# Four graph layers on one core: zero matmuls, the place of one group of transposes, and the loading of weights

## The chip, the cores and the metric

The kernel runs on one core of a Trainium2 chip. The metric is the device time of one execution in microseconds (us). One execution handles sixteen graphs.

## The reference

Sixteen graphs of 1024 nodes with 128 features pass through four layers. Each layer first normalizes its input over the features and applies relu, and adds its output to its input. The adjacency matrix is sparse (about 1.6% of the entries and the diagonal are above zero) and comes as a dense matrix of floats.

```python
# layer 0: neighbour sums over the adjacency, divided by its row sums, then one linear map of [h, sums]
h = jnp.maximum(_layernorm(x), 0.0); x = x + relu(concat(h, (adj.T @ h) / degree) @ W0.T + b0)
# layer 1: the same sum with adj / row sums, one linear map, leaky relu
h = jnp.maximum(_layernorm(x), 0.0); x = x + leaky(((adj / degree) @ h) @ W1.T + b1)
# layer 2: two rounds of message passing, with a score for every pair of nodes
h = jnp.maximum(_layernorm(x), 0.0)
for l in range(2):
    a, b = h @ We1[l, :D], h @ We1[l, D:]
    hid = relu(a[:, None, :] + b[None, :, :] + be1[l])
    scores = sigmoid(hid @ We2[l] + be2[l])
    messages = (adj * scores) @ h
    y = h + relu(concat(h, messages) @ Wu1[l] + bu1[l]) @ Wu2[l] + bu2[l]
    h = layernorm(y) * gamma[l] + beta[l]
x = x + h
# layer 3: attention over the neighbours, softmax((Wh1 + Wh2.T) * (adj + I)), elu
```

## The kernel before

**Lanes.** The work of one graph is cut into three Python generators. `first` (lane a) does layers 0 and 1, the norm ahead of layer 2, and the lists of neighbours (`build`). `main` (lane m) does the two rounds of layer 2. `last` (lane c) does the second update of layer 2 and layer 3. While graph b is in `main`, graph b-1 is in `last` and graph b+1 in `first`. `weave` takes the next piece from the generator whose share of its expected time is smallest: each yields an estimate in us, divided by MAIN_US, FIRST_US or LAST_US. That gives the order in which instructions are written down. A scheduler then orders them on each engine by priority and its own estimate of readiness, and allots tiles from pools; each engine runs its own queue in order.

**Layer 2.** A pair of node blocks that share edges is gathered (`gather`, L1015) by matmuls of a one-hot matrix (`on`, `om`) with the two linear parts (`part`) into the PSUM tile `pre`, which has two buffers. ACT takes its relu (L1031), and DVE the rest that half precision loses (L1032); both are in the tile `hid`. `dots` (L1048) multiplies `hid` by the score weights into `sc`; `scores` transposes it (`pt`) and spreads it on the edges (`val`); `scatter` (L1131) turns this into the matrix `p`, DVE multiplies it by the adjacency (`upd`), and `message` (L1148) adds products of it to one of two message sums in PSUM (`msg`, 512 columns, tags acc0 and acc1). `between` updates a half of the nodes between the two rounds (`update`: h2, xn, tx, then a norm with the power on POOL at L242 and the scaling at L365).

**Zero matmuls.** A message sum is made of many products of different widths, in an order that the lanes decide. So the sum is first set to zero by a matmul of zeros (`zero`, L563), and every product adds to it. Layer 3 does the same with its three sums per graph (`hp`, L507; tiles of 387, 387 and 258 columns).

**Norms.** `pre_ln` computes mean and variance on DVE, the power on POOL (L242), then writes the relu of the scaled rows on ACT, eight instructions (L251), and `transposed` turns them on PE (L259) through PSUM back to SBUF on ACT (L260). The last norm in `first` writes the tile `xf`; its transpose goes to a DRAM copy, which `main` reads back later.

**The start.** All weights are loaded on ACT's DMA queue ahead of everything else. Then `run` lets `first` of graph 0 go up to layer 0's own products (`bb`), calls `scaled` (which folds the signs and sizes of We2 into We1 and finds a power of two that keeps the scores in range: `bound`, `bound_t`, `unit`, `be`, `w3T`, `v`), and goes on with `first`: for each of eight row tiles of the adjacency a load of rows (`at`) and of columns (`ct`), the transposes `tn`, the neighbour products `nb`, and a write of the transposed rows to DRAM (`adjT`). Rows and columns share five buffers here.

## Time and profile before

| | value |
|---|---|
| median of three runs | 5316.95 us (5308.2 to 5318.65) |
| span of the profiled execution | 5323.4 us |
| PE busy (matmuls) | 4977.0 us, 93% |
| DVE, ACT, POOL busy | 79%, 57%, 4% |
| first 133 us: PE busy, DMA busy | 81.2 us, 64% |
| zero matmuls (L563) | 112 |

A busy time is the time in which an instruction of the engine was under way; matmuls overlap, so their busy times are longer than their share of the queue. In a timeline a row holds the start, the length, the engine and line, the tiles written and read, and in brackets the idle time of that engine before the row and what ended it. Rows with "q" behind an engine's name are DMA issues. The clock row holds the share of its full clock that TensorE was granted.

### The profile page before, as it was taken

The numbers are of one execution on the slowest core, as the hardware profiler recorded it, in microseconds if no ns is written. First come the engines' busy times: TensorE is split into PE (matmuls) and PEld (weight loads), VectorE is DVE, ScalarE is ACT, GpSimd is POOL, SyncE is SP. The second block draws the span as 40 slices with busy tenths as digits, with TensorE's granted clock in tenths as the row PEclk, the third lists the DMA queues.
The fourth block names the chain that finished last, engine by engine and source line by source line (L and its number), as shares of the span: only waits on it lengthen the run. The fifth ranks groups of instructions, "written<-read, shape, count | busy, mean of one in ns | idle before, by whom it ended". The sixth has DMA issues, their size and how long they took to land.

```text
span 5323.4 us, 112270 instructions
## 1 busy us (share of the span) xinstructions
PE 4977.0 (93%) x45109; PEld 3739.4 (70%) x45109; DVE 4216.4 (79%) x9543; ACT 3044.9 (57%) x6790; POOL 189.3 (4%) x137
## 2 busy tenths in 40 slices
PE   6999999999999999999999999999999999999986
PEld 5766777777777777777777777777767777777664
DVE  4776787877879778797887978878797887978876
ACT  5556564655646556475564756656465564755543
POOL 0000000000000000000000000000000000000000
PEclk8999999999999999999999999999999999999998
DMA  6242425243252433424334242432524334243121
GB/s 185 64 143 88 123 62 150 83 127 108 75 147 74 134 94 89 141 73 125 96 107 130 62 138 88 121 115 72 154 71 136 97 89 142 74 126 93 57 63 48
DMA packets 740130, 554.47 MB, mean 104 GB/s; under 512 B 32273, under 2 KB 686353, under 8 KB 739601
## 3 DMA queue, kind: packets, MB, share of 16 engines
q1 hardware_dynamic: 734496, 545.58, 34.4%
q8 instruction: 356, 5.83, 0.5%
q10 hardware_dynamic: 5104, 1.65, 0.1%
q14 instruction: 174, 1.42, 0.1%
HBM read 446.44 MB, written 100.66 MB: 103 GB/s over the span
## 4 chain that ended last, share of the span: by engine, by line
PE 55%; DVE 22%; ACT 12%; DMA 5%; issue 3%; POOL 2%; SPq 0%; ACTq 0%; POOLq 0%; DVEq 0%
PE pre L1015 14%; PE p L1131 7%; DVE val L1106 7%; PE nb L289 6%; PE msg L1148 5%; PE bb L297 3%; PE sc L1048 3%; DVE hid L1032 3%; DMA at<-in_adj_dram 3%; PE h L343 3%; PE hp L507 3%; ACT hid L1031 2%; PE pq L873 2%; PE pn L829 2%; DMA a<-adjT 2%
## 5 line engine op out<-in xcount | busy, mean ns | idle before, releaser
L1031 ACT ACTIVATE hid<-pre 128x320 f16<-128x320 f32 (+1 forms) x2048 | 915.6, 455 | 666.8 <-PE pre L1015 603.0
L1032 DVE SCALAR_TENSOR_TENSOR hid<-pre,hid 128x320 f16<-128x320 f32 (+1 forms) x2048 | 1006.8, 505 | 240.6 <-ACT hid L1031 227.0
L1015 PEld LDWEIGHTS <-part 128*128 128x128 f16 x8192 | 746.0, 98 | 404.8 <-issue 196.6
L1015 PE MATMUL pre<-on,part 128*128 128x320 fp8e4 (+1 forms) x4096 | 985.2, 310 | 42.7 <-DVE hid L1032 32.5
L1015 PE MATMUL pre<-om,part 128*128 128x320 fp8e4 (+1 forms) x4096 | 962.9, 309 | 0.0
L1148 PE MATMUL msg<-upd,xf 128*128 128x128 f32 (+3 forms) x3008 | 595.3, 320 | 0.3 <-DVE upd L1139 0.3
L1106 DVE TENSOR_TENSOR val<-onT,u 128x768 f32<-128x768 fp8e4 (+1 forms) x576 | 561.1, 1010 | 3.1
L1131 PE MATMUL p<-val,omT 128*128 128x128 f16 x6528 | 507.3, 219 | 23.4 <-DVE val L1106 13.4
L1131 PEld LDWEIGHTS <-omT 128*128 128x128 fp8e4 x6528 | 423.0, 96 | 89.6 <-issue 62.3
L884 ACT ACTIVATE om<-pm 128x320 fp8e4<-128x320 f32 (+1 forms) x576 | 269.8, 468 | 292.0 <-PE pm L829 289.3
L1148 PEld LDWEIGHTS msg<-upd,xf 128*128 128x128 f32 x3008 | 410.3, 192 | 15.7 <-DVE upd L1139 1.6
L1106 DVE TENSOR_TENSOR val<-omT,u 128x768 f32<-128x768 fp8e4 x448 | 410.7, 950 | 0.0
L1139 DVE SCALAR_TENSOR_TENSOR upd<-p,adj 128x512 f32<-128x512 f32 x512 | 348.9, 681 | 74.9 <-PE p L1131 69.8
L1131 PE MATMUL p<-val,onT 128*128 128x128 f16 x4480 | 375.2, 219 | 2.4 <-DVE upd L1139 2.4
L869 ACT ACTIVATE onT<-pn 128x384 fp8e4<-128x384 f32 (+1 forms) x576 | 297.9, 517 | 120.9 <-PE pn L829 97.3
L507 PE MATMUL hp<-wh,e 128*128 128x129 f32 x2048 | 330.0, 283 | 14.3 <-DVE e L503 14.0
L1069 ACT ACTIVATE srow<-sc,be_s,down 128x128 f32<-128x128 f32 (+2 forms) x512 | 256.2, 541 | 142.6 <-PE sc L1048 140.2
L1131 PEld LDWEIGHTS <-onT 128*128 128x128 fp8e4 x4480 | 304.9, 97 | 46.7 <-issue 14.5
L507 PEld LDWEIGHTS hp<-wh,e 128*128 128x128 f32 x2048 | 282.5, 193 | 48.3 <-issue 19.7
L820 DVE TENSOR_SCALAR on<-far,wid 128x384 fp8e4<-128x384 f16 (+1 forms) x576 | 242.3, 427 | 67.2 <-PE pre L1015 59.5
L1048 PE MATMUL sc<-hid,slide 128*32 128x320 f16 (+1 forms) x4096 | 281.0, 317 | 14.6 <-DVE hid L1032 10.7
L816 ACT ACTIVATE far<-iota_off,mid 128x384 f16<-128x384 f16 x448 | 273.6, 629 | 7.8 <-DVE on L820 4.8
(217 smaller groups left out, 8118.5 us busy)
## 6 DMA issues: line engine op xcount, KB each, us to landing
at<-in_adj_dram SPq DMA_DIRECT2D x128, 512.0 KB, 3.9
ct<-in_adj_dram SPq DMA_DIRECT2D x128, 512.0 KB, 4.4
adjT<-tn SPq DMA_DIRECT2D x128, 512.0 KB, 5.2
l<-adjT SPq DMA_DIRECT2D x128, 512.0 KB, 4.3
adj<-adjT SPq DMA_DIRECT2D x256, 256.0 KB, 3.6
a<-adjT SPq DMA_DIRECT2D x128, 384.0 KB, 3.3
adj<-adjT SPq DMA_DIRECT2D x448, 64.0 KB, 2.3
adj<-adjT SPq DMA_DIRECT2D x192, 128.0 KB, 2.7
```

The source lines that it names most:

```text
L289: nc.tensor.matmul(ps, mat[:, k], z[:, k], start=(k == 0), stop=(k == T - 1))
L507: nc.tensor.matmul(sums[:, t], e[:, i, t * P : (t + 1) * P], wh[:, k + i, : D + 1], start=False, stop=True, skip_group_check=True,)
L816: nc.scalar.activation(far[:, : ck * P], self.iota[t == u][:, : ck * P], AF.Abs, bias=s.mid[:, i : i + 1])
L869: nc.scalar.activation(onT, pn[:, : ck * P], AF.Copy, saturate=False)
L1015: nc.tensor.matmul(pre[:, :c], path.parts[node // Q][:, k, node % Q, v], hot[:, :c], start=(hot is on and k == 0), stop=(hot is om and k = ...
L1031: nc.scalar.activation(hid[:, 0, :c], pre[:, :c], AF.Relu)
L1032: nc.vector.scalar_tensor_tensor(hid[:, 1, :c], pre[:, :c], 0.0, hid[:, 0, :c], op0=OP.max, op1=OP.subtract)
L1048: ins = nc.tensor.matmul(self.sc[g * G : (g + 1) * G, : self.c], self.path.slide[:, self.l, G - 1 - r : 2 * G - 1 - r], self.hid[self.done ...
L1106: nc.vector.tensor_tensor(pair[:, :, :ck], right, v.rearrange("p k i o -> p i k o").to_broadcast([P, 2, ck, P]), op=OP.mult,)
L1131: nc.tensor.matmul(self.ps[d][:, i], left[:, k], halves[:, k, :, h], start=(k, h) == terms[0], stop=(k, h) == terms[-1],)
L1139: nc.vector.scalar_tensor_tensor(upd, self.ps[d], S_SCALE, self.adj[:, d * Q : (d + 1) * Q], op0=OP.add, op1=OP.mult,)
L1148: nc.tensor.matmul(self.msg[h][:, (lo - h * Q) * P : (hi - h * Q) * P], self.xf[mb // Q][:, mb % Q], up, start=False, stop=True, skip_grou ...
```

## The change

Three things are changed.

1. The zero matmuls go. The first product into a message sum or a layer-3 sum carries the start flag, and later products are ordered behind it on PE (`add_to`, with `issue_after`). The tile of zeros goes too.
2. In `first`, the last norm and its transposes are taken apart: after the norm the generator yields 5 instead of 2, and the transposes are ordered behind the gather that was written down last at that point, except for graph 0. FIRST_US goes from 115 to 118.
3. Fifteen of the weight loads move into `load_rest`, called after layer 0's own products are written down, and `scaled` is called at the ninth piece of `first` that follows, not ahead of it.

```diff
-FIRST_US = 115.0
+FIRST_US = 118.0
...
+    def load_rest():
+
+        nc.scalar.dma_start(be2_bc, be2.rearrange("l o -> o l").broadcast_to([P, L]))
+        nc.scalar.dma_start(w3_sb, w3)
...
+    def add_to(opened, dst, left, right):
+
+
+        with ExitStack() as behind:
+            if opened is not None:
+                behind.enter_context(tc.issue_after(opened))
+            ins = nc.tensor.matmul(
+                dst, left, right, start=opened is None, stop=True, skip_group_check=True
+            )
+        return ins.ins if opened is None else opened
...
-                zero(sums)
                 sums = sums.rearrange("p (t d) -> p t d", d=D + 1)
+                opened = None
...
-                            nc.tensor.matmul(
-                                sums[:, t], e[:, i, t * P : (t + 1) * P], wh[:, k + i, : D + 1],
-                                start=False, stop=True, skip_group_check=True,
+                            opened = add_to(
+                                opened, sums[:, t], e[:, i, t * P : (t + 1) * P], wh[:, k + i, : D + 1]
                             )
...
-            ps = self.psum.tile([P, HALF], F32, tag=f"acc{h}", name=name)
-            self.zero(ps)
-            return ps
-
-        def zero(self, ps):
-            nc.tensor.matmul(ps, self.zero16, self.iota2[:, : ps.shape[1]], start=True, stop=True)
+            self.opened[h] = None
+            return self.psum.tile([P, HALF], F32, tag=f"acc{h}", name=name)
...
-            yield from lane.pre_ln(xt, f"2_{name}", dst=s.xf)
-            s.xT = self.kept(lane.hT, "xT", f"xT0_{b}")
+            lane.normal(xt, s.xf, AF.Relu, f"2_{name}")
+            yield 5
+
+            with ExitStack() as behind:
+                if b:
+                    behind.enter_context(tc.issue_after(self.gathered))
+                turned = lane.transposed(s.xf, f"2_{name}")
+            yield 2
+            s.xT = self.kept(turned, "xT", f"xT0_{b}")
...
+                    path.gathered = ins.ins
...
-                    nc.tensor.matmul(
-                        self.msg[h][:, (lo - h * Q) * P : (hi - h * Q) * P],
+                    self.path.opened[h] = add_to(
+                        self.path.opened[h], self.msg[h][:, (lo - h * Q) * P : (hi - h * Q) * P],
                         self.xf[mb // Q][:, mb % Q], up,
-                        start=False, stop=True, skip_group_check=True,
                     )
...
             first = self.first(0)
             next(first)
-            self.scaled()
-            for us in first:
+            load_rest()
+            for n, us in enumerate(first):
                 if us is None:
                     break
+                if n == 8:
+                    self.scaled()
```

## The prediction

> **What bounds the kernel now.** I read the page first: engine shares, then the clock row.

> ```profile
> PE 4977.0 (93%) x45109; PEld 3739.4 (70%) x45109; DVE 4216.4 (79%) x9543; ACT 3044.9 (57%) x6790; POOL 189.3 (4%) x137
> ...
> PE   6999999999999999999999999999999999999986
> ...
> PEclk8999999999999999999999999999999999999998
> ```

> PE is busy in 4977.0 of 5323.4 us, and below nine tenths only in the first slice and the last two. In between the kernel is bound by PE's queue, which runs in order. So time can be won in three ways: fewer matmuls, fewer waits in that queue, or a shorter first slice. The change tries all three.

> Next, the groups of instructions by form, for the matmuls that only write zeros:

> ```profile
> L563 PE MATMUL msg<-iota,zero 128*128 128x512 f16 x64 | 24.5, 386 | 6.4 <-DVE w_sb L155 6.4
> L563 PE MATMUL hp<-iota,zero 128*128 128x387 f16 x32 | 10.5, 327 | 0.4 <-ACT whr L283 0.4
> L563 PE MATMUL hp<-iota,zero 128*128 128x258 f16 x16 | 4.4, 273 | 0.0
> ```

> There are 112, with 39.4 us of busy time; but busy times of pipelined matmuls overlap, so their price is from start to start, in PE's timeline. The same timeline of graph 4 shows the wait that the moved transposes cause; ACT's and POOL's timelines show its origin:

> ```profile
> 1913.28 0.38 PE L563 MATMUL msg<-iota,zero 128*128 128x512 f16 x1
> 1913.50 0.57 PE L1015 MATMUL pre<-on,part 128*128 128x480 fp8e4 x2
> ...
> 1929.72 0.43 PE L1015 MATMUL pre<-on,part 128*128 128x320 fp8e4 x2 [0.74 <-DVE hid L1032]
> 1929.99 0.43 PE L1015 MATMUL pre<-om,part 128*128 128x320 fp8e4 x2
> 1932.82 0.33 PE L259 MATMUL tp<-ident,xf 128*128 128x128 f32 x1 [2.40 <-ACT xf L251]
> ...
> 1940.92 0.33 PE L563 MATMUL hp<-iota,zero 128*128 128x387 f16 x1
> 1941.08 0.30 PE L1015 MATMUL pre<-om,part 128*128 128x320 fp8e4 x1
> ```

> ```profile
> 1932.27 3.18 ACT L251 ACTIVATE xf<-x,st 128x128 f32<-128x128 f32 x8 [1.38 <-DVE st L249]
> ```

> ```profile
> 1930.40 1.64 POOL L242 TENSOR_TENSOR st<-st,half_neg 128x8 f32<-128x8 f32 x1 [31.77 <-DVE st L239]
> ```

> A zero matmul takes 0.22 us of the queue (1913.28 to 1913.50), the 387-wide one 0.16 us. At 1932.8 PE has nothing left ahead of a transpose whose operand is not there. The granted clock then falls, as a table of stretches shows:

> ```profile
> 1929.00:1934.80 5.80, 2.68 (x18) 1.26 (x18) 3.88 (x22) 2.96 (x8) 2.60 (x2) 1.00 0.00 0
> 1934.80:1938.30 3.50, 3.50 (x18) 2.75 (x16) 3.07 (x9) 2.70 (x6) 0.36 (x1) 0.51 0.39 116
> ```

> (The columns after the length are busy PE, PEld, DVE, ACT, POOL, then clock.) Last, the DMA issues of SP at the start, and a stretch of the first layer:

> ```profile
> 17.52 0.38 SPq L732 DMA_DIRECT2D x<-in_x_dram  x1
> 38.85 0.38 SPq L691 DMA_DIRECT2D ct<-in_adj_dram  x1
> ```

> ```profile
> 40.00:75.00 35.00, 26.27 (x200) 24.88 (x199) 8.81 (x25) 12.87 (x24) 0.00 (x0) 0.80 0.98 285
> ```

> From 17.5 to 38.9 us no load is issued, since the five row buffers are full until adjacency tile 0 is transposed; after that the DMA engines are 98% busy to 75 us. What starts these loads earlier ends them earlier.

> [...]

> **The change part by part.**

> *Zero matmuls.* All 112 go, with their weight loads and one memset. 64 x 0.22 + 32 x 0.16 + 16 x 0.11 (258 of 512 columns of 0.22) = 14.1 + 5.1 + 1.8 = 21.0 us. Two lie in the wait at the start and are free. In the orders of the two built programs the counts on each engine otherwise agree. Opening products add no work: they carry a start flag. The new order edges hold later products behind the opener on PE's own queue, where they stood anyway. The opener inherits the zero matmul's wait for its bank's reader, but later. I take 20, with 15 to 39 as ends: a third absorbed by waits, or the full busy time.

> *Weights and their folding.* Counting ACT's order, the scheduler still puts 19 of the 22 first issues ahead of the first norm; three go behind the transposed copies. ACT's last three issues end at 18.57; without three (0.33 to 0.49 us each, and gaps) the norm starts about 2 us sooner. It cannot start before about 12.4, when its statistics are done. The larger gain is on PE: before, the folding chain (bound at 30.2, unit at 33.8, be at 35.6) stands ahead of tile 0's transposes at 36.5. After, they stand among the bb products, which ran from 23.6 to 29.2. So their row is free near 29 instead of 38.85: 10 us less in front of a stretch that DMA bounds. The folding moves behind the third tile's neighbour products; its chain of about 5 us (30.2 to 35.6) makes PE wait there, but five rows of 0.5 MB at 285 GB/s are 9 us of loads in flight and hide it. ACT gets three issues among its copies, 1.3 us, and SP's order changes only between transposed writes and loads. Taken: 9; ends 2 (ACT's head start alone) and 12.

> *The transposes.* Where do they stand? Before, between last layer-1 product and first transpose, PE has 5.7 us of work (xn 1.72, pre 12 x 0.2 or 0.135, tx 0.48, hp 1.34); the wait is what is missing to the operand's chain. That chain, measured: product end 1923.63, transpose 1932.82, so 9.2 us: three additions on DVE (0.35, 1.23, 1.22), statistics 1.64, small ones 0.6, the power on POOL 1.64, ACT 0.5, and other DVE work between them. After, the yield of 5 puts the whole lane one product earlier against the main lane: ACT's eight xf stand ahead of the last diagonal hid, and 7.7 us of PE work precede the transpose (one h group of 1.72 and other places). The DVE work within the chain is alike (on, hid, on: 1.45, against on, bn pieces, hid: 1.65). So the first wait shrinks to 9.2 - 7.7 = 1.5 us, where before has 0.17 + 0.91 + 2.4 = 3.5.

> But ACT now issues the diagonal hid behind eight xf (3.18 us), and DVE handles its second half behind xf of the update (L365), which waits for POOL's power of st_y (1.0 to 1.3 us). The score products sc, queued on PE right behind the seventh transpose, start with that very hid. Walked with these durations: transposes from 14.3 (counted from the first gather of the round), seventh at 16.7, DVE's hid done at 19.2: a new wait of about 2.5 us. Behind it stand the last transpose and the next gathers. Together 4.0 to 4.5 us per graph against about 4.4 before (3.5, and 0.9 between the transposes). I take 0.

> Ends: all of it gone. The fourteen windows of 20 us around these waits have a clock of 0.91 (ten) or 0.83 (four): 10 x 1.8 + 4 x 3.4 = 32 us of lost clock, plus 14 x 3.5 = 49: minus 80. Worse by 1 us and another half-clock window (1.7) each: plus 38. FIRST_US 115 to 118 only compensates the longer yields; other small shifts of the lanes: plus or minus 10, since a graph has 15 us of PE waits in all.

> Sum: 20 + 9 + 0 = 29 us. On this execution's span, 5323.4 - 29 = 5294. The three timed runs are 5308.2 to 5318.65, median 5316.95, so the forecast is 5317 - 29 = 5288.

> **Rivals.**

> *The wait mostly goes (0.25).* If DVE reaches the hid early, the sc wait vanishes, and a 1.5 us wait alone may not cost the clock: 14 x (2 + 1.1 to 2.2) = 43 to 59 more, 5229 to 5245; all gone would be 5208. For it: that is where the new edge aims. Against: the order on ACT and DVE.

> *Less than forecast (0.17).* The gain at the start is hidden by the folding chain, or the wait grows by about 1 us: 5300 to 5317.

> *Slower (0.09).* One mechanism: sc waits behind L365, and so behind POOL. The 29 us are used up from 2.1 us more per graph; with 2.5 us more of this wait, and a half-clock window each: 14 x (2.5 + 1.7) = 59, less 29: 5347.

> *The change does not do what it says:* in part it does not (19 of 22 issues stay ahead); counted above.

> **Numbers.** The likeliest case has 0.49, 5274 to 5303 on its own. The range 5235 to 5313 leaves out most of the slower case and the far end of the first rival. A measurement can tell about 0.2%, 10.6 us. Below 5306: the likeliest, the first rival and a third of the second: 0.80; within 0.2%: 0.11; slower: 0.09.

> **What would show it.** No zero matmuls; the load of 38.85 issued near 29; PE's wait before the first xf transpose near 1.5 us, and one of about 2.5 us before sc. If the second is missing and the half-clock windows are fewer than fourteen, the first rival holds; if 9 us do not appear by 130 us, the start failed.

## The result and the profile after

The changed kernel takes 5272.67 us (median of 4 runs, 5270.28 to 5277.52) against 5317.11 us (5308.2 to 5318.65) for the kernel before: ratio 0.9921 with a 95% interval of 0.9904 to 0.9938, about 44 us less by the medians and 42 by the ratio. The forecast was 29 us less. The profiled execution spans 5272.1 us, the one of the kernel before 5323.4, which is 8 us above the median of that kernel.

The page of the changed kernel, in the rows that were shown of before:

```profile
PE 4924.4 (93%) x44997; PEld 3714.9 (70%) x44997; DVE 4225.4 (80%) x9542; ACT 3069.1 (58%) x6790; POOL 199.2 (4%) x137
...
PE   6999999999999999999999999999999999999986
...
PEclk8999999999999999999999999999999999999998
```

PE has exactly 112 matmuls fewer (45109 to 44997) (PEld likewise) and DVE one memset fewer; the other counts are the same. The bound is still PE's queue, with the first slice at 6. The clock row shows nothing at this grain, though the clock turns out to matter.

The sums in PSUM now have only products among their groups (line, operation, tiles, count, then busy time, mean, and idle time in front):

```profile
L195 PE MATMUL hp<-wh,e 128*128 128x129 f32 x2048 | 334.9, 285 | 14.5 <-DVE e L515 14.3
...
L195 PE MATMUL msg<-upd,xf 128*128 128x512 f32 x256 | 135.0, 609 | 0.0
```

Opening products have taken the place of the zero matmuls: 2048 products go into `hp` and 3008 into `msg`, as many as in before, and no row of zeros is left. Why one opening product is enough for a whole sum is not shown by these traces.

SP's DMA issues at the start:

```profile
14.53 0.38 SPq L738 DMA_DIRECT2D x<-in_x_dram  x1
26.38 0.38 SPq L697 DMA_DIRECT2D ct<-in_adj_dram  x1
```

The load that before issued at 38.85 goes out at 26.38, 12.5 us earlier (foretold: near 29). The folding chain now stands behind it on PE:

```profile
24.40 0.60 PE L760 MATMUL tn<-ident,at 128*128 128x128 f32 x4
...
34.71 1.05 PE L653 MATMUL bound<-lim_x,mag 128*128 128x1 f32 x8 [1.20 <-ACT mag L649]
36.28 0.27 PE L664 MATMUL bound_t<-ident,bnd 128*2 128x128 f32 x1 [0.52 <-DVE bnd L662]
38.20 0.58 PE L681 MATMUL unit<-sel,ones 2*128 2x4 f32 x2 [1.65 <-DVE sel L675]
```

The first relu of a gathered block on ACT comes at 125.9 us, in before at 136.4: 10.5 us earlier, where the forecast had 9. Over all fourteen traces of this document it comes at 136.4 to 138.8 us with the old start and at 125.1 to 127.0 with the new one.

Last, the moved transposes, in PE's and ACT's timelines of the graph that was shown of before:

```profile
1900.93 0.57 PE L1028 MATMUL pre<-om,part 128*128 128x480 fp8e4 x2
1902.60 0.33 PE L271 MATMUL tp<-ident,xf 128*128 128x128 f32 x1 [1.10 <-ACT xf L263]
...
1904.14 0.43 PE L1028 MATMUL pre<-om,part 128*128 128x320 fp8e4 x2
1906.23 0.55 PE L271 MATMUL tp<-ident,xf 128*128 128x128 f32 x3 [1.65 <-ACT hT L272]
1907.34 0.82 PE L1062 MATMUL sc<-hid,slide 128*32 128x480 f16 x8 [0.56 <-DVE hid L1046]
```

```profile
1902.06 3.19 ACT L263 ACTIVATE xf<-x,st 128x128 f32<-128x128 f32 x8 [1.55 <-DVE st L261]
1905.15 0.55 ACT L1045 ACTIVATE hid<-pre 128x480 f16<-128x480 f32 x1
1905.60 0.58 ACT L272 ACTIVATE hT<-tp 128x512 f32<-128x512 f32 x1
```

The wait in front of the first transpose is 1.10 us (forecast 1.5). A second one is there, but not where the forecast put it: not 2.5 us before `sc`, but 1.65 us before the fifth transpose, which waits until ACT has copied the first four out of PSUM (L272, 1905.60 to 1906.18), and ACT does that behind eight `xf` and a `hid`. Before `sc` 0.56 us are left. Together 3.31 us; before had 0.74 + 2.40 = 3.14 in the rows shown, and all fourteen graphs from the third on repeat these sums within 0.03 us. The wait was split, not removed. In the graph shown half clock still follows (a granted clock of 0.55 from 1907.8 to 1911.3 us); in ten of the fourteen graphs it does not.

What the split does to the clock is worked out from the clock records of each trace, over the stretch from graph 0's first relu of a gathered block to graph 15's. "Half-clock loss" is half the length of all stretches granted less than 0.9 (the records of before and after hold 1.0 and 0.5 alone); "PE idle" is the time in which no matmul was under way, and PE's own work is what is left of the stretch without these two. Before has 39.3 and 227.9 us there, after 22.2 and 235.0. The stretch is 44.5 us shorter (4848.3 to 4803.8): 17 from the clock, minus 7 more idle, and 34.5 in PE's own work, of which the zero matmuls by their start-to-start price are 21. That leaves some 13 us of faster interleaving. With 10.5 at the start and 3.8 lost in the last graph and behind it, this is the whole difference of the two executions, 51.3 us. Between the medians it is 44 us, so some 7 us of this sum belong to the one execution of before. The clock's 17 are in part such an item: over all recorded executions the granted clock is 0.984 in before and 0.986 in the changed kernel, some 10 us of the span. The forecast lacks both the clock and the interleaving.

### The profile page after: what moved, and what is told of

Read it like the earlier page. It is cut to its first block, busy times and chain, and to the rows that moved or that the text cites. A ratio compares the mean times of both kernels' runs of the same rounds, so it can differ in the third digit from the quotient of the medians.

```text
span 5272.1 us, 112168 instructions
## 1 busy us (share of the span) xinstructions
PE 4924.4 (93%) x44997; PEld 3714.9 (70%) x44997; DVE 4225.4 (80%) x9542; ACT 3069.1 (58%) x6790; POOL 199.2 (4%) x137
## 2 busy tenths in 40 slices
PE   6999999999999999999999999999999999999986
## 3 DMA queue, kind: packets, MB, share of 16 engines
q10 hardware_dynamic: 5104, 1.65, 0.1%
## 4 chain that ended last, share of the span: by engine, by line
PE 52%; DVE 23%; ACT 13%; DMA 7%; POOL 2%; issue 2%; SPq 0%; ACTq 0%; POOLq 0%; DVEq 0%
PE pre L1028 13%; DVE val L1120 6%; PE p L1145 6%; PE nb L301 6%; PE msg L195 4%; DMA at<-in_adj_dram 4%; PE sc L1062 3%; PE h L355 3%; DVE hid L1046 3%; PE bb L309 3%; PE hp L195 3%; DMA a<-adjT 2%; PE pq L886 2%; ACT hid L1045 2%; PE pn L842 2%
## 5 line engine op out<-in xcount | busy, mean ns | idle before, releaser
L1028 PE MATMUL pre<-on,part 128*128 128x320 fp8e4 (+1 forms) x4096 | 976.2, 308 | 22.2 <-DVE hid L1046 18.2
L195 PE MATMUL hp<-wh,e 128*128 128x129 f32 x2048 | 334.9, 285 | 14.5 <-DVE e L515 14.3
L301 PE MATMUL nb<-z,l 128*128 128x128 f32 x2048 | 270.8, 282 | 26.2 <-DVE o L342 26.2
L301 PEld LDWEIGHTS nb<-z,l 128*128 128x128 f32 x2048 | 252.9, 196 | 58.5 <-DVE o L342 32.7
L889 DVE TENSOR_TENSOR omT<-pq,odd_off 128x384 fp8e4<-128x384 f32 x448 | 247.5, 552 | 47.3 <-PE pq L886 41.4
```

Of the source, the lines that this page charges most:

```text
L195: ins = nc.tensor.matmul(dst, left, right, start=opened is None, stop=True, skip_group_check=True)
L301: nc.tensor.matmul(ps, mat[:, k], z[:, k], start=(k == 0), stop=(k == T - 1))
L889: nc.vector.tensor_tensor(omT.rearrange("p (k m) -> p k m", m=P), pq[:, :ck], self.odd[t == u][:, :, None].to_broadcast([P, ck, P]), op=OP ...
L1028: ins = nc.tensor.matmul(pre[:, :c], path.parts[node // Q][:, k, node % Q, v], hot[:, :c], start=(hot is on and k == 0), stop=(hot is om a ...
```

## The experiments

Each kernel is compared with runs of the kernel before on the same chip. "Us against before" below is (ratio - 1) x 5317. PE idle and half-clock loss are those of the middle stretch of one profiled execution. Theory A of the first four is that each part brings its own share, the zeros more than their columns; B, that the surplus comes from how the scheduler interleaves everything.

**Part 1 alone, on the kernel before** (the zero matmuls go):

```diff
-                zero(sums)
+                opened = None
...
-            self.zero(ps)
+            self.opened[h] = None
```

> The kernel before with the zero matmuls replaced by opening products, and nothing else. Theory A, the zero matmuls cost more than their columns: PE's time outside idle and half-clock windows fell by 2.2 us per graph between the two traces, 35 us in all, where start-to-start prices give 21, so this kernel gains about 35 (5282 us). Theory B, they cost their columns and the rest of the 35 us belongs to the new interleaving that the other two parts bring: it gains 21 or a little less (5296 us). In both the load at 38.9 us stays, and the half-clock windows behind the xf transposes stay at about fourteen.

Measured: 5326.39 us, ratio 1.0019 (1.0012 to 1.0027): 10 us slower. Neither theory had that sign. 112 matmuls are gone and the kernel loses. The groups of `p` in before and in this kernel, from 300 to 5000 us:

```profile
L1131 PE MATMUL p<-val,omT 128*128 128x128 f16 x5944 | 463.5, 219 | 15.9 <-DVE val L1106 12.0
```

```profile
L1136 PE MATMUL p<-val,omT 128*128 128x128 f16 x5948 | 457.9, 219 | 44.7 <-DVE val L1111 44.1
```

PE's wait for DVE's `val` in front of `p` grows from 15.9 to 44.7 us. Other waits shrink, so PE idle as a whole grows from 227.9 to 241.5: 13.6 us are given back. The work on PE shrinks by 12.6 us and not by 21. The scheduler, relieved of 112 matmuls, made another order: 61% of PE's places hold the same matmul as in before.

**Part 2 alone** (norm and transposes taken apart, yield of 5, FIRST_US 118):

```diff
-FIRST_US = 115.0
+FIRST_US = 118.0
...
-            yield from lane.pre_ln(xt, f"2_{name}", dst=s.xf)
+            lane.normal(xt, s.xf, AF.Relu, f"2_{name}")
+            yield 5
...
+                    behind.enter_context(tc.issue_after(self.gathered))
```

> The kernel before with only the transposes taken apart (yield of 5, edge behind the gather, FIRST_US 118). Theory A, the wait is split and the clock keeps up: PE's idle time per graph stays within 1 us of before, but the half-clock time falls by about half, a gain of 10 to 17 us (5300 to 5307). Theory B, the fewer half-clock windows come from the other edits [...]: no gain, 5312 to 5322, with as much half-clock time as before.

Measured: 5311.33 us, ratio 0.9995 (0.9986 to 1.0003). The half-clock loss falls from 39.3 to 17.1, and PE idle rises from 227.9 to 242.7: the second takes back two thirds of the first. Theory A is right on the clock and wrong on the time.

**Part 3 alone** (weights and folding behind layer 0's own products):

```diff
-            self.scaled()
+            load_rest()
...
+                if n == 8:
+                    self.scaled()
```

> The kernel before with only the weight loads and the folding moved. Theory A: the blocked load goes out near 26 us instead of 38.9 and the first gather starts about 10 us earlier, and all of it reaches the end: 5307 us. Theory B, it is given back later, since graph 0 and graph 1 share rows and the DMA: a gain below 5 us.

Measured: 5302.32 us, ratio 0.9975 (0.9965 to 0.9986), 13 us less. Its issue on SP:

```profile
15.38 0.38 SPq L733 DMA_DIRECT2D x<-in_x_dram  x1
27.86 0.38 SPq L692 DMA_DIRECT2D ct<-in_adj_dram  x1
```

The first relu of a gathered block comes at 126.9. The order on PE is that of before in 99.9% of the places, so hardly anything else changed and the whole gain reaches the end. Theory A holds for this part.

**Parts 2 and 3, with the zero matmuls kept** (the changed kernel without part 1):

```diff
-            self.opened[h] = None
+            self.zero(ps)
...
-                opened = None
+                zero(sums)
```

> The changed kernel with the zero matmuls put back. Theory A: it loses 35 of the 44 us, 5308 us. Theory B, zeros cost only their columns: it loses 21, 5294 us. If the half-clock time also goes back up to that of before, the zeros take part in the clock as well.

Measured: 5302.73 us, ratio 0.9978 (0.9968 to 0.9988). Taking the zeros out of this kernel gives the changed one, 30 us less, between theory B's 21 and theory A's 35; taking them out of the kernel before cost 10. So the size is not a property of part 1. The half-clock loss did not go back up with the zeros: 11.9 us here, 22.2 in the changed kernel.

**Parts 1 and 3, without part 2:**

```diff
-FIRST_US = 118.0
+FIRST_US = 115.0
...
-            yield 5
...
-                    behind.enter_context(tc.issue_after(self.gathered))
```

> The changed kernel without part 2 (the last norm and its transposes as before, FIRST_US 115); parts 1 and 3 stay. Its order on PE is that of part 1 alone in all but 48 of 43,800 places. Theory S (the parts' sizes add, each with its own price): the changed kernel takes 5272.7, part 2 alone was worth 4 us, so this takes about 5277. Theory O (what counts is the order that the scheduler makes of the whole, and the zero matmuls' 21 us are won or lost with it): part 1 alone took 5326.4, and the start is worth 13, so about 5313.

Measured: 5321.3 us, ratio 1.0001 (0.9992 to 1.0009). This is 0.0018, some 10 us, less than part 1 alone, whose order it shares: the start's worth once more. Theory S is refuted: part 2, worth 3 us by itself, is worth 42 here. Theory O is right in kind, and by the ratios 4 us off in size.

**Zero matmuls of one column:**

```diff
-            nc.tensor.matmul(ps, self.zero16, self.iota2[:, : ps.shape[1]], start=True, stop=True)
+            nc.tensor.matmul(ps[:, :1], self.zero16, self.iota2[:, :1], start=True, stop=True)
```

This one happens to have part 1's order, and still opens each sum with a zero matmul, so it tells the order from the openers.

> The kernel before, in which each of the 112 zero matmuls writes one column in place of 258 to 512. In all but 3 places the order on PE is that of part 1 alone, which took 5326.4 without any zero matmul. So order and columns are those of that run, with 112 short matmuls added and the opening products and their order edges taken away. Theory O (part 1 alone lost its 21 us to its order): 112 x about 0.03 to 0.06 us more than part 1 alone, 5329 to 5333. Theory W (part 1 alone lost them since opening products wait for their bank's reader where a zero matmul waited earlier, or by the edges): the loss goes with the openers, and this takes 5317 - 20 + 5 = 5302.

Measured: 5330.93 us, ratio 1.0024 (1.0015 to 1.0034): 13 us slower than before. Its zero matmuls:

```profile
L563 PE MATMUL msg<-iota,zero 128*128 128x1 f16 x64 | 10.6, 167 | 9.1 <-DVE w_sb L155 9.1
L563 PE MATMUL hp<-iota,zero 128*128 128x1 f16 x48 | 7.9, 167 | 0.7 <-ACT whr L283 0.7
```

From start to start, with idle time behind them left out, 102 of them (those of the middle stretch) take 5.1 us of the queue, where the full ones of before take 21.7. It is 3 us slower than part 1 alone, by ratios whose intervals overlap, against 5 by that price. So the openers and their edges cost nothing that shows (Theory W would have 5302), and the order itself is what loses. Part 1's order thus shows three times what it costs over that of before: 10 + 21 = 31 us (part 1 alone), 13 + 17 = 30 (this one), 0 + 21 + 13 = 34 (parts 1 and 3, with the 13 that part 3 brought alone).

**FIRST_US alone, in the kernel before:**

```diff
-FIRST_US = 115.0
+FIRST_US = 118.0
```

> The kernel before with FIRST_US 118 in place of 115 and nothing else: no work is added or removed, only the weaving of the lanes changes; 43 per cent of the places on PE hold the same matmul as before. Theory S: no change of more than 5 us (5312 to 5322). Theory O: the order alone moves the time by 10 us or more to either side, 5297 to 5337, with the idle time of PE in graphs 1 to 15 off the 228 us of before by 10 or more.

Measured: 5335.5 us, ratio 1.0029 (1.0017 to 1.0041), 15 us slower with the same work: PE idle is 268.1 us, 40 more, and the half-clock loss only 13.7, in an execution 11 us below the median of this kernel. Theory O holds.

**The changed kernel with FIRST_US 115:**

```diff
-FIRST_US = 118.0
+FIRST_US = 115.0
```

> The changed kernel with FIRST_US 115 in place of 118: zero matmuls gone, start moved, the yield of 5 and the edge stay. 45 per cent of the places on PE hold the same matmul as in the changed kernel. Theory S: within 5 us of it (5268 to 5278). Theory O: the gain of the changed kernel hangs on its order, and another one of the same work loses part of it: 5283 to 5310, its PE idle time in graphs 1 to 15 over 245 us.

Measured: 5304.79 us, ratio 0.9973 (0.9963 to 0.9984): two thirds of the gain are gone, with the work unchanged; its PE idle is 241.1, a little under the 245 expected. The groups of the transposes, the changed kernel first, then this one (300 to 5000 us):

```profile
L271 PE MATMUL tp<-ident,xf 128*128 128x128 f32 x120 | 31.1, 306 | 38.6 <-ACT hT L272 23.1 <-ACT xf L263 15.4
```

```profile
L1062 PE MATMUL sc<-hid,slide 128*32 128x320 f16 (+1 forms) x3728 | 245.4, 315 | 41.2 <-DVE hid L1046 38.2
...
L271 PE MATMUL tp<-ident,xf 128*128 128x128 f32 x120 | 25.6, 354 | 0.3
```

Here the transposes wait for nothing at all (0.3 us), which is what the edge aims at. But `sc` waits 41.2 us (13.6 in the changed kernel). In one graph, on PE, DVE and POOL:

```profile
1911.39 0.43 PE L1028 MATMUL pre<-on,part 128*128 128x320 fp8e4 x2 [0.77 <-DVE hid L1046]
1911.66 0.43 PE L1028 MATMUL pre<-om,part 128*128 128x320 fp8e4 x2
1914.72 0.59 PE L1062 MATMUL sc<-hid,slide 128*32 128x480 f16 x8 [2.62 <-DVE hid L1046]
```

```profile
1913.74 0.17 DVE L261 SCALAR_TENSOR_TENSOR st<-st 128x8 f32<-128x8 f32 x1 [1.42 <-POOL st L254]
1913.82 0.29 DVE L243 BATCH_NORM_STATS2 bn_y<-xf 128x6 f32<-128x128 f32 x1
1914.02 0.64 DVE L1046 SCALAR_TENSOR_TENSOR hid<-pre,hid 128x480 f16<-128x480 f32 x1
```

```profile
1912.07 1.64 POOL L254 TENSOR_TENSOR st<-st,half_neg 128x8 f32<-128x8 f32 x1 [31.53 <-DVE st L251]
```

DVE stands still for POOL's power, and the `hid` that `sc` needs is queued behind it: 0.77 + 2.62 = 3.39 us, nearly the sum of before (3.14) and of the changed kernel (3.31), in a third place.

**The changed kernel without the edge:**

```diff
-                if b:
-                    behind.enter_context(tc.issue_after(self.gathered))
```

> The changed kernel without the order edge between the last gather and the transposes of the last norm; the yield of 5 and FIRST_US 118 stay. All but 183 of 43,800 places on PE hold the same matmul as in the changed kernel. Theory O (the gain of part 2 is that of the whole order, which the yield and FIRST_US decide): the same as the changed kernel, 5268 to 5278 or a ratio of 0.9913 to 0.9930. Theory E (the edge is what keeps the transposes from making PE wait, and saves half-clock windows): 10 us or more are lost, with more than eleven half-clock windows in the steady state.

Measured: 5274.88 us, ratio 0.9915 (0.9899 to 0.9932). The edge does nothing for the time in this order; Theory E falls. What acts in part 2 is FIRST_US with the yield.

**The changed kernel with FIRST_US 117, 119 and 121** (one line each, here the second):

```diff
-FIRST_US = 118.0
+FIRST_US = 119.0
```

> The changed kernel with FIRST_US 117; 54 per cent of the places on PE as in the changed kernel. Theory O: the work is the same and the order another one, so the time is a draw from the spread seen so far, 5265 to 5310, likeliest near 5290 and not near the mean of its neighbours 115 (ratio 0.9973) and 118 (0.9921). Theory T (a real optimum of lane timing near 118, which the time approaches smoothly): ratio 0.993 to 0.995.

Measured: 5284.82 us, ratio 0.9928 (0.9910 to 0.9946).

> The changed kernel with FIRST_US 119; 57 per cent of the places on PE as in the changed kernel. Theory O: a draw, ratio 0.990 to 0.999. Theory T: ratio 0.9915 to 0.9935, close to the changed kernel.

Measured: 5259.67 us, ratio 0.9891 (0.9875 to 0.9908). This version beats both kernels: its four runs (5251.78 to 5267.22) lie below the four of the version without the edge on the same chip (5272.81 to 5276.98), which has the changed kernel's time.

> The changed kernel with FIRST_US 121; 43 per cent of the places on PE as in the changed kernel. Theory O: a draw, ratio 0.990 to 0.999, so it may also beat the changed kernel. Theory T: as far off 118 as 115 is, ratio 0.995 to 0.998.

Measured: 5298.96 us, ratio 0.9960 (0.9947 to 0.9972).

From 115 to 121 the ratios are 0.9973, 0.9928, 0.9921, 0.9891, 0.9960: down to 119, then up. That is the shape of Theory T, but with the optimum at 119; its number for 117 was missed by 0.0002, that for 119 by 0.0024 (13 us). The ranges of Theory O held for 117 and 121, and that for 119 was missed by 0.0009. So these runs do not decide between a draw and a smooth optimum. In the kernel before, 115 to 118 went the other way.

**All kernels together.** In the built orders, the first transpose of `xf` stands behind 16, 20 or 24 gather matmuls of the second round:

| kernel | us against before | gathers ahead | half-clock loss | PE idle |
|---|---|---|---|---|
| before | 0 | 20 | 39.3 | 227.9 |
| part 1 alone | +10 | 20 | 35.8 | 241.5 |
| part 3 alone | -13 | 20 | 32.4 | 220.1 |
| parts 1 and 3 | 0 | 20 | 51.2 | 245.2 |
| one-column zeros | +13 | 20 | 44.4 | 237.4 |
| changed, 117 | -38 | 20 | 34.1 | 243.2 |
| changed, 115 | -14 | 24 | 34.1 | 241.1 |
| part 2 alone | -3 | 16 | 17.1 | 242.7 |
| parts 2 and 3 | -12 | 16 | 11.9 | 238.8 |
| before, 118 | +15 | 16 | 13.7 | 268.1 |
| changed (118) | -42 | 16 | 22.2 | 235.0 |
| changed, no edge | -45 | 16 | 20.5 | 234.6 |
| changed, 119 | -58 | 16 | 17.1 | 230.4 |
| changed, 121 | -21 | 16 | 18.8 | 259.4 |

The first column comes from all runs, the last two from one execution each, which lies up to 11 us from the median of its kernel (above it in before and in "parts 1 and 3", below it in "parts 2 and 3", "before, 118" and 119), so a few us in them say nothing. The half-clock loss separates without exception: 12 to 22 us where the transposes stand behind 16 gathers, 32 to 51 where they stand behind 20 or 24. The means are 17 and 39. The clock recorded for every run agrees: averaged for each kernel it is 0.983 to 0.985 with 20 or 24 gathers ahead and 0.986 to 0.988 with 16, some 15 us of the span. So the place is worth 15 to 20 us of clock. What the place changes is the length of single waits. Counted over the fourteen traces, between 140 and 4980 us, PE's gaps and whether a half-clock stretch begins near their end (from 2 us ahead of it to 5 us behind):

| gap on PE | gaps | followed by half clock |
|---|---|---|
| 2.3 us and more | 112 | 101 (90%) |
| 1.8 to 2.3 | 55 | 32 (58%) |
| 1.4 to 1.8 | 234 | 36 (15%) |
| 1.0 to 1.4 | 422 | 32 (8%) |

These gaps are not independent of each other. 70 of the 112 are the wait of 2.40 us ahead of the first `xf` transpose, in the fourteen graphs of before and of four kernels with its place, and half clock follows all of them. Fourteen are the wait of 2.62 us ahead of `sc` with FIRST_US 115, of which twelve are followed; of the other 28, 19 are. So the length of one gap does not settle it.

A finer reading of the same traces does nearly settle it. All clock changes lie on a grid of 3.41 us (within 0.01 us). For each window of this grid at full clock in the fourteen middle stretches, here is how much of it PE was busy, and whether half clock began at its end:

| PE busy in the window | windows | half clock begins at its end |
|---|---|---|
| below 40% | 95 | 95 |
| 40 to 50% | 88 | 70 |
| 50 to 60% | 266 | 22 |
| 60 to 70% | 391 | 2 |
| 70% and more | 18723 | 0 |

So of 183 windows less than half busy 165 were followed by half clock, of the 19380 others 24. Whether a wait leaves such a window depends on where the grid happens to lie. Moved through all its positions, the grid has a window less than half busy at 91% of them around the 0.74 + 2.40 us of before, and at 49% around the 1.10 + 1.65 + 0.56 us of the changed kernel. There half clock followed these waits in four graphs of fourteen; four gaps of 2.3 us and more ahead of layer 1's products (`nb`) drew it as well.

The place is not enough for a fast kernel: FIRST_US 118 in before and 121 in the changed kernel have it and pay with more PE idle: 40 us over before, and 24 over the changed kernel.

## Why the prediction was right, and which term was mis-sized

**Right.** Faster, and inside the range; 5272.7 lies 1.3 us below the likeliest case's own 5274 to 5303. *The start:* 9 forecast by the chain through the row buffer, 10.5 in the trace, 13 alone and 10 on top of part 1. The folding chain stood ahead of tile 0's transposes; behind them it costs little that shows. (An issue on ACT took up to 0.59 us in before, not 0.49; nothing rests on it.) *The transposes' wait:* forecast as moved and not removed, at 4.0 to 4.5 us against 4.4; it is 3.31 against 3.14 in the rows shown, and 3.39 where the place is another. The 4.4 was read too high: its 0.91 is 0.74 in the row, and between the transposes of before PE does not wait. The walked wait before `sc` of 2.5 us is not in the changed kernel, where the wait of 1.65 us for the copy out of PSUM takes its place, but with FIRST_US 115 it is there with 2.62. There it comes from POOL's power of this same norm (L254, then L261 on DVE), not of the update. *Transposes at 0:* alone they gave 3 us, with an interval from 7 less to 2 more.

**Luck.** That the sum was near is in part luck. Parts 1 and 3, the two that carry the forecast's 29 us, bring 0 together without part 2. With the same edits and another FIRST_US the gain is 14 (115), 38 (117), 58 (119) or 21 us (121), and nothing in the forecast says why 118 should give 42.

**Mis-sized: "other small shifts of the lanes: plus or minus 10".** The sum of the parts alone is +10 - 3 - 13 = -6 us; the whole is -42. The 36 us between are more than the forecast's whole gain. They sit in this one term: the order of one build against the other costs 31 us in part 1's, the same work spreads over 44 us between FIRST_US 115 and 121, and a constant alone, in before, costs 15. The step "I take 20" for the zeros was right about the price (21.7 us start to start, and openers whose cost does not show), but silently held all other work in its place: alone this part made the kernel 10 us slower. "In the orders of the two built programs the counts on each engine otherwise agree" was true and said nothing on that, as counts are not places.

**Also wrong: two readings of part 2.** "The yield of 5 puts the whole lane one product earlier" and "FIRST_US 115 to 118 only compensates the longer yields": FIRST_US 118 in before, without the yield, already moves the transposes from 20 to 16 gathers, and the yield without it moves them to 24. And the forecast priced the wait's sum while half clock followed the two ways of cutting it differently: the wait of 2.40 us drew half clock in all fourteen graphs, the waits of 1.10 and 1.65 in four of fourteen. That is the clock's 10 to 17 us; the first rival had counted 1.1 to 2.2 us per graph for it, and called for the wait to go, which it did not.

**Open.** Why part 1 loses 31 us in one order and the changed kernel's order loses nothing is known in part. `p`'s wait behind `val` accounts for most of part 1's new idle time, yet the changed kernel has as much of it (44.7 us from 300 to 5000 us). The traces show a second part. `sc` matmuls next to each other start 0.02 us apart on average, but the last of such a run holds the queue for 0.25 us on average. Their 3840 in the middle stretch stand in 592 runs in before, in 645 in the three kernels with part 1's order and in 558 in the changed kernel, and take 227, 244 to 245 and 218 us of the queue. So part 1's order pays 16 us for `sc` and the changed one saves 10. No run varied this alone, and the rest of the some 13 us of faster interleaving lies in differences of a few us in many groups. That the cut of the wait causes the clock gain rests on the traces; no run changed the cut alone.

## What to carry to other kernels

Where a scheduler orders the instructions, price an edit twice: its own instructions at a fixed order, and the spread between orders, which a change of one planning constant measures; here that spread was as large as the edit. After an edit, tune the constant again: 119 was worth 16 us more than 118. A wait on an in-order queue that a chain sets (3.1 to 3.4 us here, in three kernels) moves from instruction to instruction; shorten the chain, or cut the wait with work between.

## What the runs showed of the hardware

A one-column zero matmul (f16) took 0.03 us of PE's queue from start to start in 85 of 102 cases, a 512-column one 0.22. Eight `sc` matmuls that write 32 partitions each start 0.02 us apart on average when they stand side by side (0.023 in before, 0.024 in the changed kernel).
